# Largest scores by VectorE's block turns and a trip through DRAM, and later rows turned by transfers

## The chip, the cores and the metric

The kernel runs on one core of one Trainium2 chip. The metric is device time in microseconds of one execution; smaller is better. Each time given for a kernel is the median of several executions, and beside it stands one execution that the hardware profiler recorded. The core has five engines that run their own instruction streams: TensorE (PE in the profile, with its weight loads as PEld), VectorE (DVE), ScalarE (ACT), GpSimd (POOL) and SyncE (SP, which here only issues DMA transfers). Engines meet through semaphores; each works through its own list in order.

## What is computed

2048 tokens of width 256 go through one decoder layer with a causal self attention, a cross attention to 1601 context rows, a dense feed-forward part, and then a mixture of eight experts, two of them for each token. Everything is float32.

```python
def attention(Q, K, V, causal):            # scores / sqrt(256), softmax, times V
    ...
y = layernorm0(x)                          # in four blocks of 512 tokens; each block
sa = attention(y, y, y, causal=True)       # attends to all earlier rows
y = layernorm(y + sa, g1, beta1)
ca = attention(y, Z, Z, causal=False)      # Z: 1601 rows
y = layernorm(y + ca, g2, beta2)
ff = relu(y @ w1 + b1) @ w2 + b2
x = x + layernorm(y + ff, g3, beta3)
...
x = x + moe(layernorm0(x))                 # router, two of eight experts
```

As the reference has it, the four batches of the layer's setup don't matter: the input is one batch of 2048 rows, and the self attention is causal over all 2048.

## The kernel before

**Blocks.** The tokens are cut into four blocks b = 0 to 3 of TB = 512 rows, each of four tiles j of P = 128 rows. Features lie along the 256 columns of a row tile; for a matmul that contracts over features, the tile must be turned, so that features lie on partitions: y0T[b] holds the turned rows ahead of self attention (two chunks c of 128 features by 512 tokens), yT[b] the turned rows after it.

**Ahead of self attention.** `norm0(b)` (line 330) normalizes the rows of block b into y0 with VectorE and one small power on POOL for each tile (`moments`, line 224). `norm0_T(b)` (line 336) turns them: `turn_y0` calls `transpose_to` (line 252), which has PE turn two 128x128 pieces of a tile against the identity into a PSUM bank, and VectorE copy the bank to y0T. For block 0 the order is written out in `first_block`, with ACT as the copier.

**Self attention.** `self_block(b)` (line 355) runs over the key tiles kt = 0 to 4b+3. Each step issues the scores of the next tile (ss, line 364), ACT's exponential into pT (line 374), and the products with the values (acc, line 389), so PE always has the scores of kt+1 ahead of the values of kt. After the values of kt = 4b+j, tile j of the block is complete, and VectorE adds and normalizes it into ya (lines 400 to 405). Hooks, given by kt, put other work behind the values of a step: `norm0_T(b+1)` at step 1; at step 4 (step 6 for the last block) `turn_y1(b-1)`, the turn of the rows that come out of self attention. That turn doesn't use PE: `cross_over` (line 288) sends each 32-row quarter of the rows across partitions with four DMAs from SP's queue into a buffer tb, and `turn_within` (line 298) has VectorE turn 32x32 blocks of tb into yT. The buffers tb come from a pool of two.

**Cross attention.** For the last block's self attention, the cross scores of block 0 stand ahead of it. `cross_scores(b)` (line 447) makes scores for 13 tiles of context rows k (keys on partitions, 512 tokens in columns), has ACT copy each to raw[k], and VectorE keep the running maximum over k in `top`. What is left is the maximum over the 128 partitions of `top`. `largest(b)` (line 470) has PE turn the four 128x128 pieces of `top` (tt), VectorE reduce them and spread the result (wide_top). `exponentials(b)` (line 479) has PE turn wide_top back (tw), so that each column's maximum stands on all partitions, ACT copy that to top_row, VectorE subtract it from each raw[k] and ACT take the exponential. `cross_values(b)` (line 492) then multiplies with Z.

**The order of it all.** Lines 533 to 555 run self attention over the blocks. For b = 0 `norm0(1)` comes first, for b = 1 and 2 `norm0(b+1)`. In the last block, `largest(0)` stands at step 2 and `exponentials(0)` at step 4. After each block its rows are sent across (`cross_over` into tb1[b]), and `clear(b)` (line 420) writes a part of the experts' slots in DRAM, 2 MB a transfer. Lines 999 to 1004 then run, for b = 0 to 2: cross_values(b); cross_scores(b+1); the dense part ffn(b) (line 592), eight steps f of hidden and output products, with `largest(b+1)` as a hook at step 1 and `exponentials(b+1)` at step 3. The experts follow from line 1174.

**Who orders what.** PE's order is the order in which the program calls it (`manual_schedule` at line 527). VectorE's, ACT's, POOL's and SP's lists are ordered by a scheduler when the program is built, which works with estimated costs and ready times; `tc.issue_after(x)` keeps what it holds behind x. On the chip the lists are fixed.

Of the kernel before, what the change touches and what calls it, by code (L numbers as in the profile page):

```python
# [8 lines left out]
F32 = mybir.dt.float32  # L9
# [3 lines left out]
AX = mybir.AxisListType  # L13

EPS = 1e-5
P = 128
# [3 lines left out]
def xattn_ffn_moe(  # L20
# [21 lines left out]
    nc = tc.nc  # L42

    S, D = x.shape
# [4 lines left out]
    TB = 512  # L49
# [47 lines left out]
    def bank_t(name):  # L97
        return ps_t.tile([P, 512], F32, tag="t", name=name)
# [140 lines left out]
    def normalize(dst, src, name, gain=None, shift=None, whole=None, behind=None):  # L239

        mean, rs = moments(src if whole is None else whole, name)
        if gain is None:
            return scaled(dst, src, mean, rs).ins
        n = work.tile([P, D], F32, tag="n", name=f"n_{name}")
        if len(dst.shape) > 2:
            n, gain, shift = qn(n), qn(gain), qn(shift)
            src = qn(src) if len(src.shape) == 2 else src
        nc.vector.scalar_tensor_tensor(n, src, mean, gain, ALU.subtract, ALU.mult)
        with tc.issue_after(behind) if behind is not None else ExitStack():
            return nc.vector.scalar_tensor_tensor(dst, n, rs, shift, ALU.mult, ALU.add).ins  # L250

    def transpose_to(dst, src, name, copy):

        pt = bank_t(f"pt_{name}")
        for c in range(ND):
            nc.tensor.transpose(pt[:, c * P : (c + 1) * P], src[:, c * P : (c + 1) * P], ident)
        copy(dst, pt[:, : ND * P].rearrange("p (c q) -> p c q", c=ND))


# [6 lines left out]
    def row(t):  # L266
        return ya[t // TPB][:, t % TPB, :D]
# [17 lines left out]
    def crossing(name, b):  # L285
        return tbp.tile([P, TPB * D], F32, tag="tb", name=f"tb_{name}_{b}")

    def cross_over(tb, js, src):


        o, n = js[0], len(js)
        for q in range(NQ):
            last = nc.sync.dma_start(
                tb[q * Q : (q + 1) * Q, o * D : (o + n) * D], src[:, q, o : o + n, :]
            )
        return last.ins

    def turn_within(tb, b, js, behind=None):

        o, n = js[0], len(js)  # L300
        of = tb[:, o * D : (o + n) * D].rearrange("p (i j m) -> p i j m", i=NQ, j=n)
        for k, j in enumerate(js):
            to = yT[b][:, :, j * P : (j + 1) * P]
            with tc.issue_after(behind) if behind is not None else ExitStack():
                done = nc.vector.transpose(
                    to.rearrange("p c (t i) -> p i c t", i=NQ),
                    of[:, :, k, :].rearrange("p i (c r) -> p i c r", r=Q),
                )
        return done.ins

    def turned(t):
        j = t % TPB
        return yT[t // TPB][:, :, j * P : (j + 1) * P]


    y0, y0T = {}, {}

    for t in range(NT):

        y0[t] = sp.tile([P, D + 1], F32, tag=f"y0_{t}", name=f"y0_{t}")  # L320

    def ones_of(b):
        for t in range(b * TPB, (b + 1) * TPB):
# [1 line left out]

    def turn_y0(t, copy):
        b, j = divmod(t, TPB)
        transpose_to(y0T[b][:, :, j * P : (j + 1) * P], y0[t], f"y0_{t}", copy)

    def norm0(b):  # L330
        ones_of(b)
        for j in range(TPB):
            t = b * TPB + j
            normalize(y0[t][:, :D], xb[b][:, j, :], f"0_{t}")

    def norm0_T(b):
        y0T[b] = sp.tile([P, ND, TB], F32, tag=f"y0T{b}", name=f"y0T_{b}")
        for j in range(TPB):
            turn_y0(b * TPB + j, nc.vector.tensor_copy)

    def first_block():

# [77 lines left out]
    def clear(b):  # L420

        for e in range(E):
            if e // 3 == b:
                nc.sync.dma_start(
                    slots[e * NR + P : (e + 1) * NR, :].rearrange("(k p) c -> p k c", p=P),
                    empty[:, 1:, :].to_broadcast([P, REG - 1, RW]),
                )
        if b == 2:
            nc.sync.dma_start(
                slots[:DUMMY, :].rearrange("(e k p) c -> p e k c", e=E, p=P)[:, :, 0, :],  # L430
                empty[:, :1, :].to_broadcast([P, E, RW]),
            )
            nc.sync.dma_start(slots[DUMMY:, :], empty[:, 1, :])
# [4 lines left out]

    raw = cp.tile([P, NK, TB], F32, tag="raw", name="raw")
    top = cp.tile([P, TB], F32, tag="top", name="top")  # L440
    wide_top = cp.tile([P, TPB, P], F32, tag="wide", name="wide_top")
    top_row = cp.tile([P, TB], F32, tag="toprow", name="top_row")

    def keys(k):
        return P if k < KFULL else KREST

    def cross_scores(b, hooks, turns={}):
        for k in range(NK):
            n = keys(k)
            s = (bank_o if k < 2 or k % 3 == 0 else bank_s)(f"cs_{b}_{k}")  # L450
            for c in range(ND):
                nc.tensor.matmul(  # L452
                    s[:n, :],
                    lhsT=zT_sb[:, c, k * P : k * P + n],
                    rhs=yT[b][:, c, :],
                    start=(c == 0),
                    stop=(c == ND - 1),
                )
            acted.append(nc.scalar.copy(raw[:n, k, :], s[:n, :]).ins)  # L459

            if k > 0:
                topped = nc.vector.tensor_tensor(  # L462
                    top[:n, :], s[:n, :], raw[:n, 0, :] if k == 1 else top[:n, :], ALU.max
                ).ins
            if k in turns:
                turn_within(crossed[b - 1], b - 1, turns[k], topped)
            if k in hooks:
                hooks[k]()

    def largest(b):  # L470

        tt = bank_t(f"tt_{b}")
        for j in range(TPB):
            nc.tensor.transpose(tt[:, j * P : (j + 1) * P], top[:, j * P : (j + 1) * P], ident)
        m = small.tile([P, TPB], F32, tag="m", name=f"m_{b}", bufs=2)
        nc.vector.reduce_max(m, tt.rearrange("p (j k) -> p j k", k=P), axis=AX.X)
        nc.vector.tensor_copy(wide_top, m.unsqueeze(2).to_broadcast([P, TPB, P]))

    def exponentials(b):
        tw = bank_t(f"tw_{b}")  # L480
        for j in range(TPB):
            nc.tensor.transpose(tw[:, j * P : (j + 1) * P], wide_top[:, j, :], ident)
        nc.scalar.copy(top_row, tw)  # L483
        for k in range(NK):
            e = raw[: keys(k), k, :]
            nc.vector.tensor_sub(e, e, top_row[: keys(k), :])  # L486
            nc.scalar.activation(e, e, AF.Exp, scale=SCALE)
# [37 lines left out]
    ptp = selfp.enter_context(tc.tile_pool(name="ptp", bufs=4))  # L525

    ctx.enter_context(tc.manual_schedule(engines={nc.tensor.engine}))
    tb1 = {}

    def turn_y1(b):  # L530
        turn_within(tb1[b], b, ALL)

    for b in range(NB):
        if b == 0:

            with tc.issue_after(first.ins):
                norm0(1)
        elif b + 1 < NB:
            norm0(b + 1)

        def between(b=b):
            if b + 1 < NB:
                norm0_T(b + 1)

        hooks = {1: between}
        if b == NB - 1:
            cross_scores(0, {})
            hooks[2] = lambda: largest(0)
            hooks[4] = lambda: exponentials(0)
        if b > 0:  # L550
            hooks[4 if b < LAST else 6] = lambda b=b: turn_y1(b - 1)
        self_block(b, ptp, hooks)
        tb1[b] = crossing("y1", b)
        cross_over(tb1[b], ALL, quarters(b))
        clear(b)
    selfp.close()
    fp = ctx.enter_context(tc.tile_pool(name="ffn", bufs=2, side="right"))

# [33 lines left out]
    def ffn(b, js, hooks):  # L592
# [73 lines left out]
        if b < LAST:  # L666
            by_quarter = ya[b][:, :, :D].rearrange("p j (q n) -> p q j n", q=NQ)
            tb = crossing("xn", b)
            pieces = [ALL[:2], ALL[2:3], ALL[3:]]
            for some in pieces:  # L670
                sent_over = cross_over(tb, some, by_quarter)
            for some in pieces:
                turn_within(tb, b, some, normed)
            with tc.issue_after(sent_over):
                keep(b, xf)
        elif js[-1] == TPB - 1:
            keep(b, xf)
        else:
            halves.append(normed)
# [19 lines left out]
    def route(b):  # L699
        t3, t2 = three(b)  # L700
        if b == LAST:
            for j in range(TPB):
                t = b * TPB + j
                transpose_to(turned(t), row(t), f"xn_{t}", nc.scalar.copy)

        wg_of = wg_sb if b == LAST else wg_plain
        lp = bank_t(f"lp_{b}")
# [297 lines left out]

    b, H = NB - 1, TPB // 2
    cross_values(b, ALL[:H], {})
    cross_values(b, ALL[H:], {NK - 1: lambda: turned_half.append(turn_within(crossed[b], b, ALL[:H]))})
    load_xf(b)
    route_at(b - 1)  # L1010
    attn.close()
# [162 lines left out]
    with tc.manual_schedule(engines={nc.sync.engine}):  # L1174
# [7 lines left out]
            fetch_tile(n)  # L1182

    hooks = {
        2: lambda: turn_within(crossed[b], b, ALL[H:]),
        4: lambda: place_at(b - 1),
        NF - 1: lambda: [turn_tile(n) for n in range(2)],
    }
# [138 lines left out]
```

## Time and profile before

| | |
|---|---|
| median of 3 runs | 659.6 us (659.03 to 660.59) |
| the profiled execution | 660.39 us, span 658.7 us |
| PE busy | 628.7 us, 95% of the span |
| VectorE busy | 324.1 us, 49% |
| ACT, POOL busy | 143.5 us, 170.2 us |
| PE's stages | self attention of blocks 0 to 2 to 86.6 us, cross scores of block 0 to 108.9, self attention of block 3 to 160.8, cross attention and dense part to about 453, experts after that |

The profiler's views used below: rows of utilisation give the busy share of an engine in 40 equal slices of the span, in tenths (9 is 90% or more), and the clock that was granted to TensorE. A timeline lists instructions in order of time: start and duration in microseconds, engine, line of the code, operation, output and inputs by their names in the program, shape, and how many of the kind followed each other; in brackets the idle time ahead of it, with what ended it. A PE group ends a little after the next one starts, since matmuls are pipelined, so costs on PE are read from start to start. A float32 matmul shows as two records, a transpose as one.

### The profile page before, as it was taken

The page shows a single profiled execution, that of the slowest core. Times are in us where ns is not written, and L with a number is a line of the kernel's source. Part 1 is how long each engine was busy: PE and PEld are TensorE (multiplying, and loading weights), DVE is VectorE, ACT ScalarE, POOL GpSimd, SP SyncE. Part 2 cuts the span into 40 slices and gives each one's busy share as a digit, 9 for nine tenths or more (in the row PEclk, how much of TensorE's full clock was granted, in tenths as well). Part 3 has the DMA queues.
Part 4 walks back from the last instruction along what each step waited for, and adds up shares of the span by engine and source line. Part 5 has one row for each costly group of instructions (what it writes and reads, how often), then busy time and mean ns, then how long its engine had stood idle before and what let it go on. Part 6 is the DMA issues. An engine that isn't in the chain of part 4 may idle for free. (4 is left out here: it accounts for less than half of the span.)

```text
span 658.7 us, 8201 instructions
## 1 busy us (share of the span) xinstructions
PE 628.7 (95%) x2252; PEld 407.5 (62%) x2252; DVE 324.1 (49%) x995; ACT 143.5 (22%) x254; POOL 170.2 (26%) x240
## 2 busy tenths in 40 slices
PE   5999999999999999999999999999999999999980
PEld 3666654667855687467854688876565555555550
DVE  5845074134173566816686377737623434433430
ACT  2111123251023500325023420333211111111110
POOL 4312010002050021710245022443263322222231
PEclk9999999999999999999999999999999999999996
DMA  8999929001950002200212004953355555555431
GB/s 209 270 256 321 292 71 291 0 1 32 272 175 1 0 15 81 67 31 0 66 54 75 0 9 138 344 129 65 56 110 116 97 97 99 99 106 101 88 56 18
DMA packets 100559, 70.96 MB, mean 108 GB/s; under 512 B 38365, under 2 KB 94878, under 8 KB 100510
## 3 DMA queue, kind: packets, MB, share of 16 engines
q1 hardware_dynamic: 77518, 53.96, 30.5%
q0 software_dynamic: 6864, 9.08, 8.3%
q10 hardware_dynamic: 16128, 7.35, 4.0%
q8 instruction: 21, 0.34, 0.2%
q14 instruction: 28, 0.23, 0.1%
HBM read 27.98 MB, written 29.27 MB: 87 GB/s over the span
## 5 line engine op out<-in xcount | busy, mean ns | idle before, releaser
L233 POOL TENSOR_TENSOR rs<-ve,neghalf 128x1 f32<-128x1 f32 x80 | 47.9, 605 | 221.5 <-DVE ve L231 212.8
L497 PE MATMUL co<-z_sb,raw 128*128 128x257 f32 (+1 forms) x416 | 91.4, 380 | 0.0
L452 PE MATMUL cs<-yT,zT_sb 128*128 128x512 f32 (+1 forms) x208 | 90.4, 593 | 0.0
L497 PEld LDWEIGHTS co<-z_sb,raw 128*128 128x128 f32 (+1 forms) x416 | 78.7, 190 | 11.3
L452 PEld LDWEIGHTS cs<-yT,zT_sb 128*128 128x128 f32 (+1 forms) x208 | 38.5, 186 | 47.7 <-issue 46.1
L389 PE MATMUL acc<-y,pT 128*128 128x257 f32 x272 | 65.8, 382 | 2.1 <-POOL pT L376 2.1
L389 PEld LDWEIGHTS acc<-y,pT 128*128 128x128 f32 x272 | 51.1, 190 | 21.6 <-issue 11.5
L1084 PE MATMUL h_a<-wi,xT_a 128*128 x136 | 62.5, 594 | 0.0
L630 PE MATMUL fo<-w_sb,fhs 128*128 128x256 f32 x256 | 61.1, 380 | 0.0
L608 PE MATMUL fh<-yT,w_sb 128*128 128x512 f32 (+1 forms) x160 | 60.9, 508 | 0.0
L630 PEld LDWEIGHTS fo<-w_sb,fhs 128*128 128x128 f32 x256 | 48.2, 190 | 16.1 <-issue 9.3
L459 ACT COPY raw<-cs 128x512 f32<-128x512 f32 (+1 forms) x52 | 30.4, 585 | 92.0 <-PE cs L452 92.0
L486 DVE TENSOR_TENSOR raw<-raw,top_row 128x512 f32<-128x512 f32 (+1 forms) x52 | 31.7, 685 | 27.2 <-ACT top_row L483 27.2
L364 PE MATMUL ss<-y0T,y0T 128*128 128x512 f32 x96 | 44.6, 592 | 0.0
L1084 PE MATMUL h_b<-wi,xT_b 128*128 x96 | 43.3, 592 | 0.0
L374 ACT ACTIVATE pT<-ss 128x512 f32<-128x512 f32 (+3 forms) x40 | 21.3, 532 | 94.3 <-PE ss L364 94.3
L617 ACT ACTIVATE fhs<-fh,b_sb 128x512 f32<-128x512 f32 (+1 forms) x40 | 23.9, 598 | 77.4 <-PE fh L608 77.4
L1135 POOL DMA_INDIRECT out_dram<-yw_a,at_a x17 | 26.6, 1565 | 53.5 <-DVE yw_a L1133 23.6
L462 DVE TENSOR_TENSOR top<-cs,top 128x512 f32<-128x512 f32 (+1 forms) x44 | 30.2, 687 | 20.5 <-ACT raw L459 19.9
L608 PEld LDWEIGHTS fh<-yT,w_sb 128*128 128x128 f32 x160 | 29.6, 190 | 16.9 <-issue 13.1
L1084 PEld LDWEIGHTS h_a<-wi,xT_a 128*128 128x128 f32 x136 | 25.1, 190 | 21.8 <-issue 21.0
L1125 PE MATMUL y_a<-wo,gT_a 128*128 x136 | 32.5, 382 | 1.2 <-DVE gT_a L1108 1.1
(255 smaller groups left out, 732.2 us busy)
## 6 DMA issues: line engine op xcount, KB each, us to landing
slots<-empty SPq DMA_DIRECT2D x8, 2064.0 KB
wo<-in_m2T_dram SPq DMA_DIRECT2D x8, 512.0 KB
wi<-in_m1T_dram SPq DMA_DIRECT2D x4, 1024.0 KB
wi<-in_m3T_dram SPq DMA_DIRECT2D x4, 1024.0 KB
gb_b<-g_b ACTq DMA_DIRECT2D x44, 64.0 KB
gb_a<-g_a ACTq DMA_DIRECT2D x36, 64.0 KB
xs_a<-slots SPq DMA_DIRECT2D x68, 32.0 KB
tb_y<-ya SPq DMA_DIRECT2D x16, 128.0 KB
```

The source lines that it names most:

```text
L233: raised.append(nc.gpsimd.tensor_tensor(rs, ve, neghalf, ALU.pow).ins)
L364: nc.tensor.matmul(s[:, :n], lhsT=y0T[kt // TPB][:, c, (kt % TPB) * P : (kt % TPB + 1) * P], rhs=y0T[b][:, c, j0 * P :], start=(c == 0), s ...
L389: nc.tensor.matmul(acc[j][:, : D + 1], lhsT=pt[:, (j - j0) * P : (j - j0 + 1) * P], rhs=y0[kt], start=(kt == 0), stop=(kt == b * TPB + j),)
L452: nc.tensor.matmul(s[:n, :], lhsT=zT_sb[:, c, k * P : k * P + n], rhs=yT[b][:, c, :], start=(c == 0), stop=(c == ND - 1),)
L459: acted.append(nc.scalar.copy(raw[:n, k, :], s[:n, :]).ins)
L462: topped = nc.vector.tensor_tensor(top[:n, :], s[:n, :], raw[:n, 0, :] if k == 1 else top[:n, :], ALU.max).ins
L486: nc.vector.tensor_sub(e, e, top_row[: keys(k), :])
L497: nc.tensor.matmul(acc[j][:, : D + 1], lhsT=raw[:n, k, j * P : (j + 1) * P], rhs=z_sb[:n, k, :], start=(k == 0), stop=(k == NK - 1),)
L608: nc.tensor.matmul(s[:, :n], lhsT=w1_sb[:, c, f * P : (f + 1) * P], rhs=yT[b][:, c, q0 : q0 + n], start=(c == 0), stop=(c == ND - 1),)
L630: nc.tensor.matmul(acc[j], lhsT=h[:, i * P : (i + 1) * P], rhs=w2_sb[:, f, :], start=(f == 0 and i % 2 == 0), stop=(f == NF - 1), skip_gro ...
L1084: nc.tensor.matmul(into, lhsT=xT[:, c, :], rhs=wi[n, c].rearrange("p e i -> p (e i)")[:, bass.ds(w[0], I)], start=(c == 0), stop=(c == ND ...
L1125: nc.tensor.matmul(y[:, :D], lhsT=gT[:, i, :], rhs=wo[:, bass.ds(w[1] + i * D, D)], start=(i == 0), stop=(i == NI - 1),)
```

## The change

Three things, which touch each other:

- `largest` and `exponentials` no longer use PE. VectorE turns `top` in 32x32 blocks, reduces each row of a block (16 columns are left of 512), and the 128x16 result is written to DRAM and read back four times by SP's queue, so that each 32-row quarter has the four partial maxima of every column beside each other. VectorE reduces these to one, spreads it over 32 columns, and turns the 32x32 blocks back into top_row. ACT's copy is gone.
- The rows of blocks 2 and 3 ahead of self attention are turned as the later ones are: `norm0(b)` sends them across with four DMAs into a buffer tb of the same pool of two, and `norm0_T(b)` has VectorE turn 32x32 blocks. Their pieces are 64 columns wide (256 bytes). So that a feature lands on the same partition in every block, all y0T now take every second feature into a chunk; PE's transposes of blocks 0 and 1 read their tiles with a stride of two elements, and VectorE's turns of blocks 2 and 3 do so as well.
- The hook of `norm0_T(b+1)` moves from step 1 to step 6 for b = 1 and 2, `turn_y1(2)` in the last block from step 6 to step 7, and the clears move: clear(b-1) now comes behind the crossing of norm0(b+1), and clear(2) behind the last block.

```diff
     def transpose_to(dst, src, name, copy):
         pt = bank_t(f"pt_{name}")
         for c in range(ND):
-            nc.tensor.transpose(pt[:, c * P : (c + 1) * P], src[:, c * P : (c + 1) * P], ident)
+            nc.tensor.transpose(pt[:, c * P : (c + 1) * P], src[c], ident)
         copy(dst, pt[:, : ND * P].rearrange("p (c q) -> p c q", c=ND))
...
-    def turn_within(tb, b, js, behind=None):
+    def turn_within(tb, into, js, behind=None, order="p i (c r) -> p i c r"):
...
-            to = yT[b][:, :, j * P : (j + 1) * P]
+            to = into[:, :, j * P : (j + 1) * P]
...
-                    of[:, :, k, :].rearrange("p i (c r) -> p i c r", r=Q),
+                    of[:, :, k, :].rearrange(order, r=Q),
...
+    y0b = {}
+    ON_PE = 2
     for t in range(NT):
-        y0[t] = sp.tile([P, D + 1], F32, tag=f"y0_{t}", name=f"y0_{t}")
+        if t < ON_PE * TPB:
+            y0[t] = sp.tile([P, D + 1], F32, tag=f"y0_{t}", name=f"y0_{t}")
+        else:
+            b, j = divmod(t, TPB)
+            if j == 0:
+                y0b[b] = sp.tile([P, TPB, D + 1], F32, tag=f"y0b{b}", name=f"y0_{b}")
+            y0[t] = y0b[b][:, j, :]
...
     def turn_y0(t, copy):
         b, j = divmod(t, TPB)
-        transpose_to(y0T[b][:, :, j * P : (j + 1) * P], y0[t], f"y0_{t}", copy)
+        of = y0[t][:, :D].rearrange("p (m c) -> p c m", c=ND)
+        of = [of[:, c] for c in range(ND)]
+        transpose_to(y0T[b][:, :, j * P : (j + 1) * P], of, f"y0_{t}", copy)
...
     def norm0(b):
...
             normalize(y0[t][:, :D], xb[b][:, j, :], f"0_{t}")
+        if b >= ON_PE:
+            tb0[b] = crossing("y0", b)
+            by_q = y0b[b][:, :, :D].rearrange("p j (q n) -> p q j n", q=NQ)
+            return cross_over(tb0[b], range(TPB), by_q)
 
     def norm0_T(b):
         y0T[b] = sp.tile([P, ND, TB], F32, tag=f"y0T{b}", name=f"y0T_{b}")
-        for j in range(TPB):
-            turn_y0(b * TPB + j, nc.vector.tensor_copy)
+        if b < ON_PE:
+            for j in range(TPB):
+                turn_y0(b * TPB + j, nc.vector.tensor_copy)
+        else:
+            turn_within(tb0[b], y0T[b], range(TPB), order="p i (r c) -> p i c r")
...
     def largest(b):
-        tt = bank_t(f"tt_{b}")
-        for j in range(TPB):
-            nc.tensor.transpose(tt[:, j * P : (j + 1) * P], top[:, j * P : (j + 1) * P], ident)
-        m = small.tile([P, TPB], F32, tag="m", name=f"m_{b}", bufs=2)
-        nc.vector.reduce_max(m, tt.rearrange("p (j k) -> p j k", k=P), axis=AX.X)
-        nc.vector.tensor_copy(wide_top, m.unsqueeze(2).to_broadcast([P, TPB, P]))
+        nc.vector.transpose(wide_top, top)
+        m = small.tile([P, TB // Q], F32, tag="m", name=f"m_{b}", bufs=2)
+        nc.vector.reduce_max(m, wide_top.rearrange("p (n k) -> p n k", k=Q), axis=AX.X)
+        by_quarter = dram.tile([P, TB // Q], F32, tag="mq", name=f"mq_{b}", bufs=2)
+        nc.sync.dma_start(by_quarter, m)
+        tops[b] = small.tile([P, NQ, TB // Q], F32, tag="ma", name=f"ma_{b}", bufs=2)
+        for g in range(NQ):
+            nc.sync.dma_start(
+                tops[b][g * Q : (g + 1) * Q], by_quarter.rearrange("(a i) n -> i a n", i=Q)
+            )
 
     def exponentials(b):
-        tw = bank_t(f"tw_{b}")
-        for j in range(TPB):
-            nc.tensor.transpose(tw[:, j * P : (j + 1) * P], wide_top[:, j, :], ident)
-        nc.scalar.copy(top_row, tw)
+        m = small.tile([P, TB // Q], F32, tag="mm", name=f"mm_{b}", bufs=2)
+        with tc.issue_after(acted[-1]):
+            nc.vector.reduce_max(m, tops[b].rearrange("p a n -> p n a"), axis=AX.X)
+        nc.vector.tensor_copy(
+            wide_top.rearrange("p (n k) -> p n k", k=Q), m.unsqueeze(2).to_broadcast([P, TB // Q, Q])
+        )
+        nc.vector.transpose(top_row, wide_top)
         for k in range(NK):
...
         elif b + 1 < NB:
-            norm0(b + 1)
+            with tc.issue_after(norm0(b + 1)):
+                clear(b - 1)
...
-        hooks = {1: between}
+        hooks = {1 if b + 1 < ON_PE else 6: between}
...
-            hooks[4 if b < LAST else 6] = lambda b=b: turn_y1(b - 1)
+            hooks[4 if b < LAST else 7] = lambda b=b: turn_y1(b - 1)
         self_block(b, ptp, hooks)
         tb1[b] = crossing("y1", b)
         cross_over(tb1[b], ALL, quarters(b))
-        clear(b)
+    clear(NB - 2)
```

The other callers of `turn_within` and `transpose_to` are adapted to the new arguments and do what they did.

## The prediction

> **What bounds the kernel now.** I read the utilisation rows first, then the TensorE (PE) timeline where the change removes work, then VectorE's (DVE) timeline and the DMA issues beside it.
>
> ```profile
> PE   5999999999999999999999999999999999999980
> ...
> DVE  5845074134173566816686377737623434433430
> ...
> PEclk9999999999999999999999999999999999999996
> ```
>
> PE is busy 628.7 of 658.7 us; VectorE is half idle. A microsecond taken from PE's order is a microsecond of time, and so is one in which PE must wait. The transposes on PE:
>
> ```profile
> 31.24 0.60 PE L256 MATMUL pt_y<-ident,y 128*128 128x128 f32 x4
> 32.14 0.77 PE L256 MATMUL pt_y<-ident,y 128*128 128x128 f32 x4 [0.30 <-DVE y0T L257]
> 32.74 1.88 PE L364 MATMUL ss<-y0T,y0T 128*128 128x512 f32 x4
> ...
> 47.01 0.70 PE L389 MATMUL acc<-y,pT 128*128 128x257 f32 x2 [0.70 <-POOL pT L376]
> 47.55 3.60 PE L364 MATMUL ss<-y0T,y0T 128*128 128x512 f32 x8
> ...
> 56.17 0.60 PE L256 MATMUL pt_y<-ident,y 128*128 128x128 f32 x4
> ...
> 57.99 1.88 PE L364 MATMUL ss<-y0T,y0T 128*128 128x512 f32 x4
> ...
> 120.98 0.60 PE L474 MATMUL tt<-ident,top 128*128 128x128 f32 x4
> 121.42 1.88 PE L364 MATMUL ss<-y0T,y0T 128*128 128x512 f32 x4
> ```
>
> The turns of the third block (b = 2) stand early in block 1's self attention, 31.24 to 32.74: long before 47.55, where block 2 first needs them. What VectorE does meanwhile:
>
> ```profile
> 51.36 0.48 DVE L250 SCALAR_TENSOR_TENSOR ya<-n,rs,be1b 128x256 f32<-128x256 f32 x1 [0.44 <-POOL rs L233]
> 51.76 0.74 DVE L227 BATCH_NORM_STATS2 st<-x 128x6 f32<-128x256 f32 x2
> ...
> 56.93 0.40 DVE L237 TENSOR_SCALAR y<-x,mv,rs 128x256 f32<-128x256 f32 x1
> ...
> 58.20 0.42 DVE L257 COPY y0T<-pt_y 128x256 f32<-128x256 f32 x1 [0.20 <-PE pt_y L256]
> 58.54 2.07 DVE L305 STREAM_TRANSPOSE yT<-tb_y 128x256 f32<-128x256 f32 x4
> ```
>
> It finishes block 1's layer norms (to 51.8), normalizes block 3's rows (51.76 to 57.3), and only then turns block 0's y1 (58.54), although that turn is hooked into block 1's step 4 and its transfers were issued from 34.54 to 37.20. VectorE's order is a list fixed when the program is built, so a turn can stand far behind its data.
>
> **The change, part by part.**
>
> *Removed from PE.* Largest scores: the four tt groups and the four tw groups cost what they push back the next matmul: 120.98 to 121.42 and 128.32 to 128.76, 0.44 us each, alike in the other blocks; 8 x 0.44 = 3.52. The turns of blocks 2 and 3: 32.74 - 31.24 = 1.50 and 57.99 - 56.17 = 1.82. Together **-6.84 us**.
>
> *Added to VectorE: where the new turn stands.* In the changed program's instruction order VectorE has, after block 1's last layer norm: norm0(3) whole, the four turns of block 0's y1, and then the four turns into y0T of block 2. PE's first block-2 scores wait for the last of these. PE's side: 47.55 less the 1.50 removed, 46.05. VectorE's side: its layer norms follow PE, so they too move up by 1.50. In norm0(3) the last y starts at 56.93 behind a copy that is gone; its 1/std is there 0.72 after the variance (53.68 against 52.96 for the first tile), so 55.88 + 0.72 = 56.60, moved up: 55.10. The y1 turns start 0.33 later (the pitch of that row), 55.43; four take 2.07 with a pitch near 0.475, so the new four start at 57.33 and end at 59.40; with 0.06 to PE (its first score follows the ACT copy by that much at 9.33) PE starts at 59.46. It stands idle 59.46 - 46.05 = **13.4 us**. The new turns read every second element; the trace has no such read. Lower bound 0 more (same form as 58.54); upper: the strided write of this same operation makes 627 ns of the 402 of L1066, as much again adds 4 x 0.22 = 0.9. I take 0, the row with the same shape.
>
> Is the data there? Its four DMAs follow the y1 ones (34.54 to 37.20) on SP, so 37.2 to 39.9, ahead of the 6 MB of slot clears, which now come after. The DMA engines were busy 0.12 of the time between 33 and 35 us: little is ahead. That hides this transfer and its 2048 packets of 256 B; 57.33 leaves 17 us.
>
> *PE after the pause.* Nowhere does this trace pause PE for 13 us in mid-run. The nearest row is the opening:
>
> ```profile
> 9.33 5.97 PE L364 MATMUL ss<-y0T 128*128 128x512 f32 x8 [0.46 <-ACT y0T L257]
> 15.13 1.90 PE L389 MATMUL acc<-y,pT 128*128 128x257 f32 x8
> ```
>
> 5.80 us for four records of 512 columns and four of 384. Later these go at a pitch of 0.43 (1.72 for four at 114.08 to 115.80) and 0.32 (1.29 for four at 152.91 to 154.20): 3.0. So PE's first work ran at half pace and lost 2.8 us, though the granted clock shows 1.00 there. Bounds 0 and 2.8; I take **2.8**, the one case of PE coming out of idleness.
>
> The Trainium skill (TensorE: Matmul & The Clock Gate, Part 1) speaks against this change here: an idle window of about 3.4 us halves the clock, and about 3.4 us of busy time restores it. By that page the loss would be an estimated 1.7 us and the sum 1.1 lower; the opening's 5.8 us at half pace is longer than the page's window, and the measurement counts.
>
> *Block 3's turn* costs nothing: its scores come only after cross_scores(0), 22 us of PE (86.60 to 108.92). In VectorE's order it takes the place that block 1's y1 turn had (86.20, 2.02 us); that one moves up into VectorE's idle time before 80.62. Cover gone, it would cost its 2.0 us.
>
> *The trip through DRAM.* After the last maximum (ffn of block 0: 206.50, ending 207.19) come a 128x512 turn (0.70 by L1108), a reduction (0.69), a write, four reads, a small reduction (about 0.2), a copy (0.43) and a turn (0.70); then the subtractions. A DMA issue takes 0.6 (9.04 for 12), and the last of twelve issued by 251.32 was used at 252.72, 1.4 later. Write 2.0, four reads 4 x 0.6 + 1.4: about 6 us, bounds 4 (overlapped) and 9 (a 512 KB write released its follower only 3.1 after issue, twice that plus the issues). So subtractions start at 208.6 + 6 + 1.4 = 216.0, against 222.87 now: earlier. Who waits: on ACT, by the new order, six exponentials stand before relu 4 and seven before relu 5 (now one and seven, a step later). Thirteen subtractions take 7.92, so the last exponential ends near 224.7 and relu 5 near 225.4. PE wants relu 5 at 227.21 - 0.88 = 226.33: 0.9 to spare. I take 0; at 9 us of trip each of three ffn blocks loses about 2, **0 to +6**.
>
> For block 0 the SP queue has a 2 MB clear between the write and the reads: 6.5 us at 325 GB/s. With everything 12.9 later by then (-1.50 + 13.4 + 2.8 - 1.82), the write issues near 125, the reads land near 135, subtractions start at 136.5, and step 6's exponential is wanted by 146.0 behind six exponentials (4 us): 5 us of cover. The clears themselves end some 35 us later; the first rows put into the slots come after 270. Block 3's crossing waits on SP for the first clears to land, near 60, and is used after 91. POOL's queue isn't passed by anything moved.
>
> *Neither here nor there.* VectorE loses eight copies of 0.415 and gains eight turns near 0.52, in idle time; ACT loses four copies of 0.585. Block 1's PE transposes now load every second element as weights: no row for it; 0 to +1.1 (eight loads at twice 0.141), 0 taken.
>
> **Sum.** -6.84 + 13.4 + 2.8 = +9.4 on the profiled execution's 660.39 (span 658.7): 669.8. The median of the runs is 659.6, 0.8 lower, so **669.0 us**.
>
> **Rivals.**
> - *No pause; the removed transposes decide* (the other side): 659.6 - 6.84 = 652.8. It needs the turns into block 2's y0T done by 46.05, hence ahead of block 1's layer norms on VectorE. For: VectorE is idle from 33.4 to 41.6 and the rows could cross in that time. Against: the built order, and the y1 turn of the trace that already stood so late. Below a pause of 6.84 minus the restart it would be a gain. 6%.
> - *The trip isn't hidden*: pause as forecast and about 2 us in each ffn block, 669.0 + 6 = 675. For: 0.9 us to spare on ACT. Against: earlier subtractions than now. It decides from a trip of about 7 us. 14%.
> - *The crossing is late too*: were block 2's rows to land only with the first clears, near 60 (40 plus 6.3 MB at 325 GB/s), the turns would end at 62.1 rather than 59.4 and more if the reads are slow: 672 to 674. Against: issued ahead of the clears. 6%.
>
> **How the numbers follow.** Forecast 74%, with its own range 665.5 (no restart loss, 0.7 less pause) to 670.9 (strided reads and weights). The range takes in most of the second and third rivals: **665.5 to 675**. Faster by over 0.2%: 0.06; within 0.2% (about what runs here can tell): 0.01, since a pause of just 4 us has no mechanism; slower: 0.93.
>
> **What would show it.** A single PE gap of 13 us near 46 us, released by a VectorE turn into y0T; the first scores after it at double length; tt and tw gone, and the 0.44 steps with them; no PE wait before cross_values; relu 4 and 5 just before PE wants them. No gap at 46 us would make the forecast wrong at its root; gaps of 1 to 2 us at steps 4 and 5 of each ffn would show the trip.

## The result and the profile after

The changed kernel takes 667.75 us (median of 6 runs, 666.84 to 669.32) where the kernel before takes 659.32 (median of 6, 658.07 to 660.59): ratio 1.0133, 95% interval [1.0113, 1.0152]. It is slower by 8.4 us; the forecast was 669.0, in 665.5 to 675. The profiled execution took 667.19, its span is 665.4 against 658.7 before.

The first view is the utilisation rows of the changed kernel's page: 40 slices of 16.6 us each, the busy share in tenths.

```profile
PE   6974999999999999999999999999999999999981
...
DVE  5745035350546635954768646837733433443330
...
PEclk9996999999999999999999999999999999999996
```

One slice stands out, the fourth: PE falls from 9 to 4, and the granted clock from 9 to 6. All the others are as full as before. The list of PE's waits names it (engine, tile and line, the releaser, then us in total, how often, and the longest):

```profile
PE ss L382 <- DVE y0T L305: 13.0, 1, 13.0
```

It is one wait of 13.0 us, for a VectorE turn into y0T. PE's timeline and VectorE's show both sides of it (start, duration, engine, line, operation, tiles; in brackets the idle time before the first instruction of the group and what ended it):

```profile
45.56 0.70 PE L407 MATMUL acc<-y,pT 128*128 128x257 f32 x2 [0.70 <-POOL pT L394]
59.30 5.29 PE L382 MATMUL ss<-y0T,y0T 128*128 128x512 f32 x8 [13.04 <-DVE y0T L305]
64.42 1.90 PE L407 MATMUL acc<-y,pT 128*128 128x257 f32 x8
```

```profile
49.91 0.48 DVE L250 SCALAR_TENSOR_TENSOR ya<-n,rs,be1b 128x256 f32<-128x256 f32 x1 [0.44 <-POOL rs L233]
50.31 0.75 DVE L227 BATCH_NORM_STATS2 st<-x 128x6 f32<-128x256 f32 x2
...
55.15 0.41 DVE L237 TENSOR_SCALAR y<-x,mv,rs 128x256 f32<-128x256 f32 x1 [0.73 <-POOL rs L233]
55.48 1.98 DVE L305 STREAM_TRANSPOSE yT<-tb_y 128x256 f32<-128x256 f32 x4
57.30 1.94 DVE L305 STREAM_TRANSPOSE y0T<-tb_y 128x256 f32<-128x256 f32 x4
```

VectorE goes through its list in order: block 1's last layer norm ends at 50.4, norm0(3) runs from 50.31 to 55.5, then block 0's y1 turns, and only from 57.30 the four turns that PE has been waiting for since 46. None of the last three groups waits for a transfer (no bracket names a DMA). The order is what is late.

After the pause, eight score records take 59.30 to 64.42, 5.12 us. Eight such records later in the same trace take 119.74 to 123.18, 3.44:

```profile
119.74 3.60 PE L382 MATMUL ss<-y0T,y0T 128*128 128x512 f32 x8
123.18 1.90 PE L407 MATMUL acc<-y,pT 128*128 128x257 f32 x8
```

So 1.68 us are lost to a slow restart. The table of stretches shows the granted clock beside it (window, length, busy time of PE, PEld, DVE, ACT and POOL, clock, DMA share, GB/s):

```profile
50.00:55.00 5.00, 0.00 (x0) 0.00 (x0) 3.49 (x16) 0.00 (x0) 2.04 (x4) 0.50 1.09 338
55.00:60.00 5.00, 0.70 (x1) 0.50 (x2) 4.10 (x9) 0.00 (x0) 0.12 (x1) 0.50 1.10 317
60.00:65.00 5.00, 5.00 (x11) 2.29 (x10) 0.00 (x0) 0.91 (x2) 0.00 (x0) 0.75 1.15 290
65.00:70.00 5.00, 5.00 (x20) 3.47 (x19) 2.03 (x4) 0.88 (x2) 0.00 (x0) 1.00 1.21 277
```

The clock is 0.50 in the pause and 0.75 in the first full stretch after it: about half of that still ran at half pace. In stretches of 0.25 us the clock falls to 0.50 at 48.9, some 2.6 us after PE went idle, and is back at 1.00 at 62.5, 3.2 us after PE resumed; half of 3.2 is 1.6, the loss.

The trip through DRAM is hidden. In the dense part of block 0, VectorE shows how long it took, ScalarE (ACT) what stands behind it, PE whether anyone waits:

```profile
217.92 0.69 DVE L494 TENSOR_REDUCE m<-wide_top 128x16 f32<-128x512 f32 x1
223.27 0.26 DVE L506 TENSOR_REDUCE mm<-ma 128x16 f32<-128x64 f32 x1 [4.66 <-DMA ma<-mq]
```

```profile
230.50 3.74 ACT L514 ACTIVATE raw<-raw 128x512 f32<-128x512 f32 x7
234.14 0.67 ACT L647 ACTIVATE fhs<-fh,b_sb 128x512 f32<-128x512 f32 x1
```

```profile
236.29 1.89 PE L660 MATMUL fo<-w_sb,fhs 128*128 128x256 f32 x8
```

The trip took 4.66 us. Relu 5 (L647), behind seven exponentials, ended at 234.81, and PE took it up at 236.29 with no idle time before it: 1.5 us to spare. For block 0, whose trip has a 2 MB clear in it, the wait was 9.82 us and PE did not wait either.

One gain had not been forecast. Where block 2's self attention ends, the two traces differ on POOL. First before, then after:

```profile
85.10 0.65 POOL L233 TENSOR_TENSOR rs<-ve,neghalf 128x1 f32<-128x1 f32 x1 [1.46 <-DVE ve L231]
...
85.72 0.29 POOL L376 TENSOR_SCALAR_AFFINE_SELECT pT<-pT 128x128 f32<-128x128 f32 x1
...
86.06 0.70 PE L389 MATMUL acc<-y,pT 128*128 128x257 f32 x2 [0.70 <-POOL pT L376]
```

```profile
95.10 2.02 DVE L305 STREAM_TRANSPOSE y0T<-tb_y 128x256 f32<-128x256 f32 x4
...
96.54 0.29 POOL L394 TENSOR_SCALAR_AFFINE_SELECT pT<-pT 128x128 f32<-128x128 f32 x1 [1.29 <-ACT pT L392]
```

Before, the mask of the last pT stood behind an inverse square root of a layer norm on POOL, and PE waited 0.70. After, VectorE is at block 3's turns just then (95.10), sends POOL no variance, and the mask starts as soon as ScalarE's exponential is there. PE's wait is gone: three such waits (2.1 us) before, two (1.4) after.

*The account.* Against before, PE starts block 2 at 59.30 instead of 47.55 (+11.75), cross_scores(0) at 97.43 instead of 86.60 (+10.83), ffn(0) at 215.64 instead of 205.68 (+9.96). In terms: -1.45 for block 2's transposes, +13.2 pause (59.30 against a start at 46.10), +1.68 restart, -1.82 for block 3's transposes, -0.7 for POOL's mask: +10.9 at cross_scores(0). Two tt and tw groups less at 0.44 make +10.0 at ffn(0); six more leave +7.4 at the end, against +6.7 in the spans. PE's last group starts 7.1 later (648.63 instead of 641.52), so of the last 0.7 some 0.3 lies among the expert tail's small waits on PE and 0.4 behind PE's work; neither is settled.

### The profile page after: what moved, and what is told of

It is laid out like the page before. It is cut to its first block, busy times and chain, and to the rows that moved or that the text cites. A ratio compares the mean times of both kernels' runs of the same rounds, so it can differ in the third digit from the quotient of the medians.

```text
span 665.4 us, 8146 instructions
## 1 busy us (share of the span) xinstructions
PE 624.9 (94%) x2204; PEld 403.6 (61%) x2204; DVE 330.8 (50%) x1007; ACT 141.6 (21%) x250; POOL 170.1 (26%) x240
## 5 line engine op out<-in xcount | busy, mean ns | idle before, releaser
L382 PE MATMUL ss<-y0T,y0T 128*128 128x512 f32 x96 | 46.3, 611 | 13.0 <-DVE y0T L305 13.0
L647 ACT ACTIVATE fhs<-fh,b_sb 128x512 f32<-128x512 f32 (+1 forms) x40 | 24.0, 599 | 81.7 <-PE fh L638 81.7
L638 PEld LDWEIGHTS fh<-yT,w_sb 128*128 128x128 f32 x160 | 30.0, 190 | 17.5 <-issue 13.4
L382 PEld LDWEIGHTS ss<-y0T,y0T 128*128 128x128 f32 x96 | 18.8, 197 | 28.9 <-issue 13.9
L394 POOL TENSOR_SCALAR_AFFINE_SELECT pT<-pT 128x128 f32<-128x128 f32 x16 | 4.9, 305 | 113.8 <-ACT pT L392 113.8
```

Of the source, the lines that this page charges most:

```text
L382: nc.tensor.matmul(s[:, :n], lhsT=y0T[kt // TPB][:, c, (kt % TPB) * P : (kt % TPB + 1) * P], rhs=y0T[b][:, c, j0 * P :], start=(c == 0), s ...
L638: nc.tensor.matmul(s[:, :n], lhsT=w1_sb[:, c, f * P : (f + 1) * P], rhs=yT[b][:, c, q0 : q0 + n], start=(c == 0), stop=(c == ND - 1),)
L647: nc.scalar.activation(h[:, :n], s[:, :n], AF.Relu, bias=b1_sb[:, f : f + 1]).ins
```

## The experiments

They were run in three groups, on more than one chip. With largest_alone, rows_alone and trip_longer the kernel before took 659.4 us (658.46 to 659.88), as above. With the other two groups it took 665.44 (661.37 to 667.45) and 666.17 (663.18 to 669.07); those are read by their ratios. On these two slower chips every version profiled shows small PE waits in block 3's dense part (1.3 to 2.9 us in which nothing recorded holds PE, or 0.9 to 4.3 for a relu) that the first chip's traces lack. The kernel before was not profiled there, and the cause of these waits stays open.

### The two halves of the change

*largest_alone*: only the largest scores go by VectorE and DRAM; the rows are turned on PE as before.

```diff
 (the kernel before)
-        tt = bank_t(f"tt_{b}")
...
+        nc.vector.transpose(wide_top, top)
...
+        nc.sync.dma_start(by_quarter, m)
...
-        tw = bank_t(f"tw_{b}")
...
+        nc.vector.transpose(top_row, wide_top)
```

> The kernel before with the new largest and exponentials alone; the rows ahead of self attention are turned on PE as before. Theory (the trip is hidden and eight transpose groups of 0.44 us go): 659.3 - 3.5 = 655.8, no new PE wait before cross_values or in the dense part. Rival (the trip costs in the dense part): about 2 us in each of three blocks, 660 to 662.

Measured: 655.48 us (4 runs), ratio 0.9938 [0.9921, 0.9954], and no new PE wait. This half gains 3.9 us; the forecast from the 0.44 us steps was 3.5.

*rows_alone*: only the rows of blocks 2 and 3 cross; the largest scores stay on PE.

```diff
 (the changed kernel)
-        nc.vector.transpose(wide_top, top)
...
+        tt = bank_t(f"tt_{b}")
...
-        nc.vector.transpose(top_row, wide_top)
+        tw = bank_t(f"tw_{b}")
...
```

> The changed kernel with the old largest and exponentials (transposes on PE, copy on ACT): only the rows of blocks 2 and 3 are turned by transfers and VectorE. Theory (the two parts add up): 667.75 + 3.5 = 671.3, that is 12 us above the kernel before, with the same pause of 13 us and the same slow restart. Rival (the parts help each other): differs by over 1.5 us from 671.3.

Measured: 671.13 us (4 runs), ratio 1.0174 [1.0154, 1.0193], with the pause in full:

```profile
58.73 6.65 PE L382 MATMUL ss<-y0T,y0T 128*128 128x512 f32 x8 [13.05 <-DVE y0T L305]
65.22 1.90 PE L407 MATMUL acc<-y,pT 128*128 128x257 f32 x8
```

The whole loss is in this half. The halves add up: -3.9 + 11.7 = +7.8, against +8.4 for the whole. The restart took 6.49 us for the eight records here, so it lost 3.05.

### Is it the place in VectorE's list?

*turn_before_norm0_3*: norm0(3) is issued behind the turns into block 2's y0T; block 1's layer norms stay ahead.

```diff
 (the changed kernel; done_T[b] holds what turn_within returns for y0T[b])
...
-            with tc.issue_after(norm0(b + 1)):
+            with tc.issue_after(done_T[2]) if b == 2 else ExitStack():
+                sent = norm0(b + 1)
+            with tc.issue_after(sent):
                 clear(b - 1)
```

> Only block 3's first normalization is put behind the turns into y0T of block 2; they still come behind block 1's layer norms. Theory (the pause is the list's work ahead of the turns, microsecond for microsecond): the turns of y1 and y0T start at 50.3 instead of 55.5, so the pause shrinks by 5.2 to about 7.8 us; the restart costs about 1.7 as before: 667.75 - 5.2 = 662.5. Rival (data late): pause unchanged, 667.75. Rival (the restart shrinks with the pause): 661.5 or less.

PE's timeline:

```profile
54.14 6.15 PE L382 MATMUL ss<-y0T,y0T 128*128 128x512 f32 x8 [7.88 <-DVE y0T L305]
60.13 1.90 PE L407 MATMUL acc<-y,pT 128*128 128x257 f32 x8
```

The pause is 7.88 us instead of 13.04: 5.2 less, the length of norm0(3). The ratio is 1.0034 [1.0013, 1.0056] (10 runs, 667.98 us on a slower chip). What is left of the pause is the end of block 1's layer norms, the y1 turns and the four turns into y0T themselves. The slow restart stays (5.99 us for eight records), though the pause is shorter.

*turn_first*: the turns are hooked at step 3 of block 1, and block 1's four layer norms are issued behind them.

```diff
 (the changed kernel)
...
-        hooks = {1 if b + 1 < ON_PE else 6: between}
+        hooks = {1 if b + 1 < ON_PE else 3 if b == 1 else 6: between}
...
-                nc.vector.reciprocal(r, acc[j][:, D : D + 1])
+                with tc.issue_after(done_T[2]) if b == 1 else ExitStack():
+                    nc.vector.reciprocal(r, acc[j][:, D : D + 1])
```

> VectorE's four turns into y0T of block 2 are put ahead of block 1's layer norms (hook at step 3, and the layer norms of that block's four tiles issue behind the turns). Theory (the place in VectorE's list makes the pause, and the pause makes the lost clock): rows land near 40.5, turned by 42.5, PE reaches block 2 at 46.1 without a wait; the pause of 13.0 and the 1.7 us of restart both go: 667.75 - 14.7 = 653.0, PE's wait on y0T under 1 us. Rival (the rows themselves come late): the turns end at 57 or later wherever they stand in the list, the pause stays near 13 us and the time within 2 us of 667.75. Rival (the layer norms pushed back become the new wait): a PE wait of 2 to 4 us at the first values of block 2, 655 to 657.

VectorE's timeline, and PE's:

```profile
40.18 2.04 DVE L305 STREAM_TRANSPOSE yT<-tb_y 128x256 f32<-128x256 f32 x4 [8.59 <-DMA tb_y<-ya]
43.86 2.01 DVE L305 STREAM_TRANSPOSE y0T<-tb_y 128x256 f32<-128x256 f32 x4 [1.65 <-DMA tb_y<-y]
```

```profile
45.93 3.70 PE L382 MATMUL ss<-y0T,y0T 128*128 128x512 f32 x8 [0.29 <-DVE r L419]
49.46 1.90 PE L407 MATMUL acc<-y,pT 128*128 128x257 f32 x8
```

Now the turns wait for their transfer, not for VectorE's list: the rows are there at 43.86, 4.6 us after the last of their DMAs was issued (36.54 + 2.71) and 3.4 later than expected. PE waits 0.29 us (the bracket names the reciprocal that follows the turns on VectorE; the turns themselves end at 45.87), nothing waits for the layer norms that were pushed back, and the eight records take 3.53: pause and slow restart are both gone. One more of the 0.7 us waits on POOL's mask is gone too, at the end of block 1, where VectorE is now at these turns. It takes 658.96 us (6 runs) on a slower chip, ratio 0.9904 [0.9882, 0.9926].

*after_again and turn_first_again*: the changed kernel and this version, run again on one chip.

> The changed kernel unaltered, for a comparison on one chip with the version that turns block 2's rows first. Theory (the 13 us PE pause and the slow restart are the loss): ratio to the kernel before 1.013, that is 667.7 us where the kernel before takes 659.4; the pause again 13.0 us at 46 us, the first eight score records between 5.1 and 6.5 us long.

> The changed kernel with block 2's turns hooked at step 3 and block 1's layer norms issued behind them. Theory: no PE gap over 1 us near 46 us and first scores at full length (3.5 to 3.7 us for eight records), so 667.7 - 13.0 - 1.7 = 653.0 on a chip where the kernel before takes 659.4: ratio 0.990, and to the changed kernel 0.978. Rival (part of the loss lies elsewhere, as in the DRAM trips or strided weights): over 655.

Measured: 672.47 us (670.62 to 672.96, 6 runs), ratio 1.0108 [1.0075, 1.0141], and 656.9 us (656.03 to 659.37, 6 runs), ratio 0.9879 [0.9844, 0.9913]. The one is 15.6 us under the other, a ratio of 0.977 as expected (0.978). PE's wait was 13.04 in the changed kernel and 0.25 in the other; the granted clock from 50 to 60 us was 0.50 against 1.00. Moving the turns in VectorE's list turns a loss of 1.1 to 1.3% into a gain of 1.0 to 1.2%, with all other parts of the change as they were. By the ratio to the kernel before, that is the fastest version run.

### How much is the restart?

*pe_kept_busy*: 14 products that nobody uses are put on PE ahead of block 2's first scores.

```diff
+        if b == 2:
+            warm = bank_t("warm")
+            for n in range(14):
+                nc.tensor.matmul(
+                    warm, lhsT=y0T[0][:, 0, :P], rhs=y0T[0][:, 0, :], start=(n == 0), stop=(n == 13)
+                )
         p = scores(0)
```

> The changed kernel, with 14 more 128x512 products on PE between block 1 and block 2 (12.0 us of PE work, whose result nothing reads). Theory (the slow first scores behind the pause are TensorE's clock, lowered by idleness): the eight score records behind the pause take 3.4 us instead of 5.1, granted clock 1.00 throughout, 667.75 - 1.7 = 666.0. Rival (they are slow because of what they read): 5.1 us again and 667.75.

```profile
45.16 12.18 PE L429 MATMUL warm<-y0T 128*128 128x512 f32 x28
58.42 3.70 PE L382 MATMUL ss<-y0T,y0T 128*128 128x512 f32 x8 [1.08 <-DVE y0T L305]
61.95 1.90 PE L407 MATMUL acc<-y,pT 128*128 128x257 f32 x8
```

PE still cannot start block 2 before the turns, but it is not idle, and the eight records take 3.53 us, with a granted clock of 1.00 in every stretch from 45 to 65 us. So the slow restart comes of the idle time, and not of the y0T that it reads. The ratio is 1.0099 [1.0077, 1.0121] (6 runs). This execution's profile has one of the slower chips' waits in block 3's dense part, 4.3 us for a relu; against the changed kernel's 1.0108 on the later run the total alone would not tell the restart apart; the records do.

### Would the crossing have been late behind the clears?

*turn_first_clears_ahead*: turn_first, with the 6 MB of slot clears issued ahead of the crossing, as the kernel before has them.

```diff
 (turn_first)
...
-            with tc.issue_after(norm0(b + 1)):
-                clear(b - 1)
+            sent = norm0(b + 1)
...
         cross_over(tb1[b], ALL, quarters(b))
-    clear(NB - 2)
+        clear(b)
```

> As turn_first, but the clears of the slots go back to where they stood before the change: each behind its block's crossing, so clear(0) is ahead of block 2's rows on SP's queue. Theory (the rows must cross ahead of 6 MB of clears): the rows land near 58, the turns end near 60, the pause is back at about 14 us and the time at 667 to 670, although the turns stand first in VectorE's list. Rival (the DMA engines serve both side by side, so the order of issue matters little): within 2 us of turn_first, near 653.

SP's DMA queue (start, time over which the group was issued), VectorE, and PE:

```profile
36.30 10.67 SPq L443 DMA_DIRECT2D slots<-empty  x3
47.07 11.81 SPq L293 DMA_DIRECT2D tb_y<-y  x4
```

```profile
63.44 1.97 DVE L305 STREAM_TRANSPOSE y0T<-tb_y 128x256 f32<-128x256 f32 x4 [21.77 <-DMA tb_y<-y]
```

```profile
65.47 6.13 PE L382 MATMUL ss<-y0T,y0T 128*128 128x512 f32 x8 [21.04 <-DVE r L419]
```

Ratio 1.0217 [1.0193, 1.0241] (4 runs), a PE pause of 21.0 us: worse than either theory had it. The expectation put the landing at about 58 from the clears' bytes alone. In fact the four issues themselves, 2.7 us long in the changed kernel (36.16 to 38.87), took 11.8 behind the clears, and the rows landed at 63.4. So the part of the change that moves the clears behind the crossing is needed: without it the best place in VectorE's list is worth nothing.

### How well is the trip hidden?

*trip_longer*: one more copy from DRAM to DRAM in each trip.

```diff
+        first = dram.tile([P, TB // Q], F32, tag="mf", name=f"mf_{b}", bufs=2)
-        nc.sync.dma_start(by_quarter, m)
+        nc.sync.dma_start(first, m)
+        nc.sync.dma_start(by_quarter, first)
```

> The changed kernel with one more copy from DRAM to DRAM in each trip of the largest scores. The trip took 4.66 us from the reduction to the first partial maxima used; one more copy should add about 2 to 2.5. Theory (the cover is what ACT's list leaves: relu 5 ended at 234.81 and PE wanted it at 236.29, 1.5 us): each of the three dense parts loses 0.5 to 1 us, 669.3 to 670.8, with PE waits on relu 5. Rival (the cover is wider, the exponentials only have to be there for cross_values): 667.75.

Measured: 668.73 us (4 runs), ratio 1.0138 [1.0119, 1.0157], the same as the changed kernel's. The trip took 6.50 us, 1.8 more, and no relu made PE wait. My expectation fell, and ScalarE's timeline shows why:

```profile
227.77 1.24 ACT L516 ACTIVATE raw<-raw 128x512 f32<-128x512 f32 x2 [0.43 <-DVE raw L515]
230.10 0.69 ACT L649 ACTIVATE fhs<-fh,b_sb 128x512 f32<-128x512 f32 x1 [1.09 <-PE fh L640]
230.69 3.74 ACT L516 ACTIVATE raw<-raw 128x512 f32<-128x512 f32 x7
234.32 0.67 ACT L649 ACTIVATE fhs<-fh,b_sb 128x512 f32<-128x512 f32 x1
234.90 2.18 ACT L516 ACTIVATE raw<-raw 128x512 f32<-128x512 f32 x4
```

Ahead of relu 4 there are now two exponentials instead of six, and four were put behind relu 5. The list is made when the program is built, with the longer trip in view; the cover moves with the trip.

*trip_six*: six more copies.

> The changed kernel with six more copies from DRAM to DRAM in every trip of the largest scores; one more copy took the trip of a dense part from 4.66 to 6.50 us, so six should make it about 15.7, and block 0's from 9.8 to about 21. Theory (the list of ScalarE, built with the longer trip in view, puts the exponentials behind relu 6 instead of ahead of relu 4 and 5, and cross_values starts late enough to hide them): no PE wait on a relu, 668 to 669.5 us, ratio 1.013 to 1.016. Rival (the cover is the fixed 1.5 us that relu 5 had to spare): about 9 us lost in each of three dense parts, near 695.

Measured: 681.63 us (4 runs), ratio 1.0238 [1.0192, 1.0284], 9.2 over the changed kernel on the same chip. The trip took 16.7 us. Neither theory holds: the rival's 27 us are not there, since all but one exponential now stand behind relu 7 and relus 4 to 6 are waited for nowhere; but the cover has an end. PE's timeline at the start of cross_values(1) and of block 3's dense part, and the stretch of the second:

```profile
243.08 1.03 PE L529 MATMUL co<-z_sb,raw 128*128 128x257 f32 x4
245.42 14.81 PE L529 MATMUL co<-z_sb,raw 128*128 128x257 f32 x66 [1.31 <-DVE yb L688]
...
418.51 1.85 PE L747 MATMUL lp<-wg_plain,yT 128*128 128x8 f32 x16
422.08 3.78 PE L643 MATMUL fh<-yT,w_sb 128*128 128x256 f32 x8 [1.72 <-DVE yT L305]
425.65 1.91 PE L665 MATMUL fo<-w_sb,fhs 128*128 128x256 f32 x4
```

```profile
420.00:430.00 10.00, 8.29 (x28) 6.85 (x28) 8.31 (x33) 1.65 (x4) 4.35 (x8) 0.66 0.88 295
```

VectorE adds fo into yb only behind its 13 subtractions, so PE waits for it in two blocks (1.31 and 1.05). PE also waits for block 3's turned rows (1.72; VectorE's turn had itself waited 1.41 for their transfer), and in block 3's dense part 1.3 more than in the changed kernel on that chip (3.45 for a relu, against 1.26 that nothing recorded holds and 0.92 for a relu). After the 1.72 the clock is low again: the eight fh records take 3.57 us and four fo records 1.71, where the same later take 1.72 and 0.86, about 2.7 lost. Together that is about 8 of the 9.2; the rest, and what delays block 3's relu, stay open.

## Why the prediction was right, and where it was off

- *Removed transposes, -6.84.* Right: 1.45 at block 2, with 1.82 for block 3 the starts add up to within 0.1, two steps of 0.44 go between cross_scores(0) and ffn(0), and largest_alone gains 3.9 for its 3.52.
- *The pause, +13.4.* Right, and the deciding step: PE would start block 2 at 59.46 by the forecast; it did so at 59.30. The order of the list gave it, and turn_before_norm0_3 and turn_first showed that the place in the list makes it: the pause shrinks by norm0(3)'s length, then disappears.
- *Strided reads, 0.* Right: the four turns with every second element took 1.94 us, the four without 1.98 (over the trace's eight such turns a median of 606 ns each, over twelve without 624). Block 1's strided weights, also taken as 0, cost at most 0.06 us: a load went from 140 to 199 ns, but it lies beside the products (the scores behind them start at 20.80 instead of 20.74).
- *The restart, +2.8.* The mechanism was right, the size too high for this execution: 1.68. Over the seven profiled executions with a pause that PE spent idle it was 1.6 to 3.05, so the size is not one number, and 2.8 lies within it. pe_kept_busy and turn_first showed that it goes with the idleness. The Trainium skill (TensorE: Matmul & The Clock Gate, Part 1) has a clock restored by about 3.4 us of busy time, which makes the loss an estimated 1.7. Three executions agree (1.68, 1.68, 1.63); the others lost 2.5 to 3.05, which is 5 to 6 us at half pace and not 3.4. The granted clock bears this out: in the seven it came back 3.1 to 6.0 us after PE resumed, and half of that time is each one's loss to within 0.1. It fell 1.5 to 2.6 us after PE went idle, sooner than the idle window that the prediction names. What sets the moment of its return is open.
- *The trip, about 6 us, hidden.* Hidden, as taken; its size was 4.66, so relu 5 had 1.5 to spare instead of 0.9. The issue of a read was taken as 0.6, where the row named for it gives 0.75 (9.04 for 12); the four reads in fact went out in 1.76, 0.44 each. The step that was wrong in the rival is its price: 2 us for each dense part from a trip of 7. At 6.50 nothing was lost, because the list is rebuilt round the trip; at 16.7 it was 9.2 in all, by other waits than the relus'.
- *What the sum left out:* the 0.7 on POOL, a wait that lay on PE's path before and that the new order removes. With the restart (-1.1), the pause (-0.2) and the unsettled 0.7 it accounts for the 2.7 by which the spans' +6.7 lies below the forecast's +9.4; between medians the difference is +8.4, since the execution profiled before lay 1.1 above its median and the one after 0.6 below.
- *Rivals.* No pause, 652.8: this is what turn_first makes of the change (0.9879 and 0.9904 of 659.3 is 651 to 653), and the condition named for it, turns ahead of block 1's layer norms, is the one that decided. Crossing late: it was not, in the changed kernel; clears_ahead shows that the mechanism is real and its price higher than the 3 to 5 us of the rival.

## What to carry to other kernels

Moving work off the bound engine pays only if the result stands early enough in the other engine's list: read where the built order puts the new instruction and what stands ahead of it, and do that before counting the microseconds saved. A transfer that a later stage needs goes ahead of bulk transfers on its queue, and a layer norm that nobody awaits yet goes behind the turn that PE awaits. A long pause of the bound engine can cost more than its length: behind the seven pauses of 7.9 to 21 us here the work started at half pace.

## What had not been expected of the hardware

- After a PE pause of 7.9 to 21 us the granted clock was 0.50, until 3.1 to 6.0 us after PE resumed, and the first eight records took 5.1 to 6.5 us instead of 3.44: 1.6 to 3.05 us lost, differing between executions and not growing with the pause (5.99 after 7.88, 5.12 after 13.04, 5.97 after 21.04).
- In trip_six a wait of just 1.72 us was followed by such a stretch, with a clock of 0.66 over ten microseconds; ahead of it stood 1.85 us of products of 8 columns, and the clock fell 0.4 us into the wait. In the wait of 3.45 us at 446.3 to 449.7, with products of 256 columns ahead of it, the clock stayed at 1.00, and the records behind it went at full pace (0.97 us for four, then 0.86). Why the one and not the other is open; no run here tests it.
- In the opening, eight records take 5.8 us although the granted clock shows 1.00 there, before as after.
- Four small issues on SP's queue took 2.7 us with no bulk transfer ahead of them and 11.8 behind 6 MB of clears.
